# Moving normalisation, last sums and the tanh of a convolution-attention kernel to other engines

## The chip, the cores and the metric

The kernel runs on one core of one Trainium2 chip, all in fp32. The metric is the device time of one execution in microseconds (us), as a median of several runs. The engines are named PE (TensorE), ScalarE (ACT), VectorE (DVE), GpSimd (POOL) and SP (the DMA queue).

## The reference

Eight images of 128 channels by 36 x 36 pixels go through two layers. This is what the changed places compute, cut from the reference:

```python
# layer 0: x = x + conv_attn(groupnorm(x)); only a_x, the first half of the stack, reaches h
x = conv1x1(inp, w_x) + b_x
attn = softmax(einsum('ancq,bncd->anbqd', q, k), axis=-1)      # 1296 queries, 1156 keys
a_x = einsum('bncd,anbqd->anbcq', v, attn)
h = tanh(conv1x1(concat([x, a_x]), w_h) + b_h)
out = conv1x1(h, w_o) + b_o
# layer 1, tokens t = pixels: additive attention
q, k = x @ Wq.T + bq, x @ Wk.T + bk                            # x = layernorm(t)
scores = einsum('bijd,d->bij', tanh(q[:, :, None] + k[:, None]), w) + bw
t = t + softmax(scores) @ x
# then a gated mixture of 64 experts on layernorm(t): per image and expert the top 8 tokens
logits = layernorm(t) @ gate_w.T + gate_b
```

The additive attention is by far the most work: 1296 x 1296 pairs of tokens times 128 channels of tanh, for each image.

## The kernel before, in words

**The main loop.** The kernel turns each tanh of a sum into a quotient: exponentials of sums and differences of channels are made once per token ("features"), matmuls over them give a denominator and a numerator for pairs of tokens, and the sum over channels is a sum of numerator over denominator. An image is cut into 3 query chunks of 432 and 11 key tiles (ten of 128, a remainder of 16). A query chunk with a key tile is a *unit*. A full unit has 12 *slots*, a remainder unit 3; an image has 33 units or 369 slots, the whole kernel 2952. In a slot PE makes two numerators (`n`, in a pool of four PSUM buffers) and, three slots ahead (`LAG`), two denominators (`d`, a pool of two); ScalarE takes the logarithm of the denominators (L815) and, for two slots at a time, the exponential of its negative (L818); VectorE multiplies it with the numerators (L835 to L846); GpSimd adds up two thirds of the products (`accp`, L851 and L853) and VectorE the rest (`accd`).

**Everything else is background.** The other work is written as Python generators that give way after each step. A step is put either at the start of a slot (`step`, `TAKE`: work for VectorE, ScalarE, GpSimd) or behind its matmuls (`matmuls`: work for PE), and says how many slots to rest. Four lanes hold them: the next query features, the attention's end (`attend`) with the last image's gate, the gate of the image before (`gating`), and the background proper, which prepares the next image: `normal`, `conv_keys`, `layer0`, `tokens`, `keys`. `matmul_turn` lets background matmuls in against a budget of `PACE` columns a slot; unused budget is not saved beyond one slot's. The order on each engine is fixed when the program is built, and every engine works its own list in order. The first image's preparation runs before the loop with nothing beside it (`drain`); the experts run after it.

**The places that are touched.**
- `layer0`: for each chunk of 432 queries ten score tiles are exponentiated, five pairs of matmuls give `pa`, summed on VectorE into `ax` (L395, L397). Then `pt` holds the softmax sums, ScalarE makes their reciprocal `ri` by a logarithm and an exponential (L405, L406), and VectorE multiplies and adds `px` into `hpre` (L412, L413). After the third chunk one tanh takes all of `hpre`, which needs another table of functions than the loop's:

```python
            yield step(2)
            nc.scalar.activation(hp, hp, AF.Tanh, bias=hb)
            nc.scalar.preload_act_table_set(LNEXP)
            yield matmuls(2)
```

- `tokens`: transposes bring `r` into token rows (`tpl`), VectorE copies them to `tok`, eleven pairs of statistics follow (L525, L526), GpSimd takes the power -1/2 (L218) and normalises eleven tiles (L538), two per step; then they are transposed back (`tpc`).
- `attend`: each of twelve pieces per image is summed in two halves of PSUM, added in `sums` (L625, L628), and divided and added to the residual by L631, whose inputs `sums` and `t2` lie in SBUF.
- `gate_logits`: twelve tiles are transposed and stored (`tt`), normalised on GpSimd (L681), transposed again and multiplied by the gate. For the last image this is done chunk by chunk.

Of the kernel before, what the change touches and what calls it, by code (L numbers as in the profile page):

```python
# [15 lines left out]
N = H * W  # L16
# [5 lines left out]
T = 108  # L22
# [35 lines left out]
DVE_PAIRS = (2, 5, 8, 11)  # L58
PACE = 370

# [4 lines left out]
def kernel(  # L65
# [55 lines left out]
    with ExitStack() as loop, ExitStack() as score:  # L121
# [83 lines left out]
        hb = const.tile([C, 1], F32, tag="hb", name="hb")  # L205
        nc.vector.tensor_add(hb, ph[:, :1], bh_s)

        LNEXP = "natural_log_exp_and_others"
# [21 lines left out]
        def matmuls(rest=0):  # L230
            return (True, rest)
# [97 lines left out]
        def layer0(b):  # L329
# [16 lines left out]
            for g in range(0, NDT, 4):  # L346
# [14 lines left out]
                yield matmuls()  # L361
            hp = big_tile("hpre")[:, :N]
            for c in range(NCH):
# [12 lines left out]
                for o, n in DTILES:  # L376
# [8 lines left out]
                    yield matmuls()  # L385
                ax = chunk_tile("ax0")
                for j0 in range(0, NDT, 2):
                    pa = aux("pa0")
                    for j in (j0, j0 + 1):
                        n = DTILES[j][1]  # L390
                        bmm(pa[:, :CH], vw[:n, j, :], ex[j][:n], start=(j == j0), stop=(j > j0))
                    yield TAKE
                    if j0 == 0:
                        total(NDT - 1)
                        nc.vector.tensor_scalar(ax, pa[:, :CH], 1.0 / D, None, ALU.mult)  # L395
                    else:
                        nc.vector.scalar_tensor_tensor(  # L397
                            ax, pa[:, :CH], 1.0 / D, ax, ALU.mult, ALU.add
                        )
                    yield matmuls()  # L400
                pt = aux("pt0")
                bmm(pt[:, :CH], ones[:DT], tot[:DT], start=True, stop=True)
                yield TAKE
                ri = chunk_tile("ri0")
                nc.scalar.activation(ri, pt[:, :CH], AF.Ln, scale=1.0 / D)  # L405
                nc.scalar.activation(ri, ri, AF.Exp, scale=-1.0)  # L406
                yield matmuls(1)
                px = aux("px1")
                bmm(px[:, :CH].rearrange("p (a b) -> p a b", b=W), wh_s[:, 0, :],
                   xpad[:, 1 + c * RC : 1 + (c + 1) * RC, 1 : 1 + W], start=True, stop=True)  # L410
                yield TAKE
                nc.vector.tensor_mul(ax, ax, ri)  # L412
                nc.vector.tensor_add(hp[:, cols], px[:, :CH], ax)  # L413
                yield matmuls()
            yield step(2)
            nc.scalar.activation(hp, hp, AF.Tanh, bias=hb)
            nc.scalar.preload_act_table_set(LNEXP)
            yield matmuls(2)
            for c in range(NCH):
                cols = slice(c * CH, (c + 1) * CH)  # L420
                po = aux("po0")
                bmm(po[:, :CH], wo_s, hp[:, cols], start=True, stop=True)
                yield TAKE
                nc.vector.scalar_tensor_tensor(
                    r[:, cols], po[:, :CH], bo_s, r[:, cols], ALU.add, ALU.add
                )
                yield matmuls()
# [63 lines left out]
        def tokens(b):  # L491
# [42 lines left out]
            nc.gpsimd.memset(xh[:, :, C : C + 1], 1.0)  # L534
            yield step()
            for t in range(NKT):
                n = KT[t][1]
                nc.gpsimd.tensor_scalar(  # L538
                    xh[:n, t, :C], tok[:n, t, :], mv[:n, t, 0:1], rs[:n, t : t + 1],
                    ALU.subtract, ALU.mult,  # L540
                )
                if t % 2 == 1:
                    yield step()
            xT = big_tile("xT")[:, :N]
# [56 lines left out]
        def attend(b, c, es):  # L601
# [8 lines left out]
            for i in range(TPC):  # L610
# [3 lines left out]
                for some in (range(6), range(6, NKT)):  # L614
# [9 lines left out]
                    if j < NKT - 1:  # L624
                        nc.vector.tensor_copy(sums, pa)  # L625
                        yield matmuls()
                    else:
                        nc.vector.tensor_add(sums, pa, sums)  # L628
                inv = small.tile([T, 1], F32, tag="inv", name="inv")
                nc.vector.reciprocal(inv, sums[:, C : C + 1])  # L630
                nc.vector.scalar_tensor_tensor(  # L631
                    t2[:T, at, :], sums[:, :C], inv, t2[:T, at, :], ALU.mult, ALU.add
                )
# [15 lines left out]
        def gate_logits(b, chunks):  # L649
# [499 lines left out]
```

## Time and profile before

| What | us |
|---|---|
| median of 3 runs (lowest, highest) | 6428.76 (6428.02, 6435.07) |
| profiled execution, its own time | 6428.41 |
| its span in the trace | 6426.7 |
| before the first slot | 188 |
| an image in the loop, images 0 to 6 | 763 to 768 |
| the last image | 685 |
| after the last slot | 194 |

Starts and lengths of slots are read from the logarithms L815 in the trace. The profile's busy times say how long an engine had something under way; a matmul that waits in the pipe counts as busy, so PE's share is an upper bound. A group's row gives instructions of one line and shape, their number, total and mean, and then the idle time of the engine in front of them with what ended it. The clock is what the throttle granted PE, 1.00 being full speed. Rows "so many us, [idle, who]" of the timeline merge neighbours of one line.

### The profile page before, as it was taken

Reading aid. Unit: us, or ns where it says so; the run is one execution under the profiler, and the core shown is the slowest. Engines: PE = TensorE matmul, PEld = TensorE weight load, DVE = VectorE, ACT = ScalarE, POOL = GpSimd, SP = SyncE. Lnnn points to the kernel's source line nnn. Section 1 sums busy time; section 2 is a strip of 40 time slices with the busy share of each in tenths; the row PEclk is TensorE's granted clock in tenths of the full one; section 3 lists DMA queues with packets and bytes.
Section 4 is the critical chain, followed back from the end, with each engine's and each line's share of the span. In section 5 each row is a group of like instructions: output and inputs, shape, how many; then the busy total and the mean of one; then the engine's idle time right before and its main releaser. Section 6 shows DMA issues by size and latency. Waiting matters only on the chain.

```text
span 6426.7 us, 106771 instructions
## 1 busy us (share of the span) xinstructions
PE 6054.8 (94%) x40448; PEld 2813.9 (44%) x40448; DVE 4900.4 (76%) x9315; ACT 5354.6 (83%) x5426; POOL 4798.1 (75%) x2966
## 2 busy tenths in 40 slices
PE   8999999999999999999999999999999999999986
PEld 4444444444444444444444444444444444544432
DVE  3687778877788777888788887887778877778862
ACT  1788898888888888888888888888888888989970
POOL 3677777787777877777787787778777787888870
PEclk9999999999999999999999999999999999999997
DMA  0200011000110002100111001100011000100017
GB/s 28 66 31 23 22 63 36 30 24 27 56 46 19 24 27 68 33 26 22 44 47 38 22 23 53 43 32 25 20 63 43 23 24 27 61 26 28 24 66 253
DMA packets 155284, 265.78 MB, mean 41 GB/s; under 512 B 53712, under 2 KB 79824, under 8 KB 154768
## 3 DMA queue, kind: packets, MB, share of 16 engines
q1 hardware_dynamic: 154768, 258.95, 12.5%
q8 instruction: 318, 5.21, 0.3%
q14 instruction: 198, 1.62, 0.1%
HBM read 196.81 MB, written 61.83 MB: 40 GB/s over the span
## 4 chain that ended last, share of the span: by engine, by line
PE 67%; DVE 12%; ACT 7%; issue 7%; POOL 6%; DMA 1%; SPq 0%; POOLq 0%; DVEq 0%; ACTq 0%
PE n L793 30%; PE d L793 10%; PE pc L237 7%; PE pa L237 6%; ACT lq L815 5%; DVE n L840 3%; DVE rp L846 3%; PE s L237 3%; PE pk L237 3%; PE pq L237 2%; DVE accd L842 2%; POOL accp L853 2%; DVE t L631 1%; PE n L800 1%; POOL t L681 1%
## 5 line engine op out<-in xcount | busy, mean ns | idle before, releaser
L853 POOL TENSOR_TENSOR accp<-accp,rp 128x864 f32<-128x864 f32 x1464 | 2965.2, 2025 | 1028.0 <-DVE rp L846 975.3
L793 PE MATMUL n<-qf,kf 32*128 32x432 f32 (+1 forms) x11520 | 3239.2, 579 | 93.4 <-DVE rp L846 47.0
L815 ACT ACTIVATE lq<-d 128x864 f32<-128x864 f32 x2952 | 2552.6, 882 | 690.7 <-PE d L793 643.3
L793 PE MATMUL d<-qf,kf 32*128 32x432 f32 (+1 forms) x11520 | 2876.6, 568 | 21.2 <-ACT lq L815 16.4
L846 DVE TENSOR_TENSOR rp<-n,lq 128x432 f32<-128x432 f32 x3984 | 2202.6, 600 | 623.7 <-PE d L793 399.3
L818 ACT ACTIVATE lq<-lq 128x1728 f32<-128x1728 f32 x1488 | 2429.0, 1632 | 47.1
L793 PEld LDWEIGHTS n<-qf,kf 32*128 32x128 f32 (+1 forms) x11520 | 1167.1, 187 | 1703.4 <-DVE rp L846 586.3
L793 PEld LDWEIGHTS d<-qf,kf 32*128 32x128 f32 (+1 forms) x11520 | 1038.8, 188 | 392.2 <-issue 254.1
L840 DVE TENSOR_TENSOR n<-n,lq 128x432 f32<-128x432 f32 x1440 | 811.7, 608 | 280.1 <-PE n L793 239.2
L842 DVE TENSOR_TENSOR accd<-n,accd 128x432 f32<-128x432 f32 x1440 | 867.4, 602 | 24.7
L851 POOL TENSOR_TENSOR accp<-rp 128x864 f32<-128x864 f32 x264 | 533.8, 2022 | 221.1 <-DVE rp L846 217.5
L237 PE MATMUL pa<-xh,e 128*108 128x129 f32 x1920 | 262.6, 284 | 55.6 <-DVE rp L846 34.7
L860 POOL TENSOR_TENSOR accp<-accp 128x432 f32<-128x432 f32 x264 | 290.8, 1101 | 16.2
L237 PEld LDWEIGHTS pa<-xh,e 128*108 128x108 f32 x1920 | 223.3, 175 | 179.1 <-DVE rp L846 107.4
L594 POOL TENSOR_SCALAR qf<-qf,cs_s 128x432 f32<-128x432 f32 x192 | 262.7, 1374 | 42.0 <-ACT qf L593 42.0
L863 POOL TENSOR_TENSOR accd<-accp,accd 128x432 f32<-128x432 f32 x240 | 265.6, 1107 | 28.5 <-DVE accd L842 10.4
L237 PE MATMUL s<-q,k 128*116 128x432 f32 x480 | 229.8, 570 | 3.3 <-DVE q L260 2.1
L237 PEld LDWEIGHTS pk<-xT,a_k 128*128 128x128 f32 x1408 | 172.2, 193 | 109.8 <-DVE accd L842 27.6
L374 POOL TENSOR_TENSOR tot<-tot,e 116x432 f32<-116x432 f32 x192 | 212.0, 1104 | 6.1
L835 DVE TENSOR_TENSOR accd<-n,lq 128x432 f32<-128x432 f32 x240 | 144.9, 604 | 91.6 <-PE n L793 60.5
L381 ACT ACTIVATE e<-s 116x432 f32<-116x432 f32 x240 | 125.0, 521 | 106.6 <-PE s L237 105.5
L237 PE MATMUL pk<-xT,a_k 128*128 128x128 f32 (+1 forms) x1408 | 203.2, 288 | 2.6 <-DVE accd L842 2.3
(175 smaller groups left out, 4144.4 us busy)
## 6 DMA issues: line engine op xcount, KB each, us to landing
kf<-kd SPq DMA_DIRECT2D x240, 512.0 KB
kd<-ks SPq DMA_DIRECT2D x160, 256.0 KB
w<-in_weight_dram SPq DMA_DIRECT2D x32, 1024.0 KB
x<-in_x_dram SPq DMA_DIRECT2D x8, 648.0 KB
t<-tokd SPq DMA_DIRECT2D x96, 54.0 KB
t2d<-t2T SPq DMA_DIRECT2D x24, 216.0 KB
res<-t2d SPq DMA_DIRECT2D x8, 648.0 KB
out_dram<-res SPq DMA_DIRECT2D x8, 648.0 KB
```

What stands on the lines that cost most here:

```text
L237: mm(out, lhsT, rhs, **kw)
L594: nc.gpsimd.tensor_scalar(qf[:, 1, :], qf[:, 0, :], cs_s[:, q : q + 1], None, ALU.mult)
L793: mm(outs[h][:, :CH], kf[rows[h], q, :], qf_of[b, c, q][rows[h], part, :], start=True, stop=True)
L815: nc.scalar.activation(lq[:, o : o + 2, :], d[:, :, :CH], AF.Ln)
L818: nc.scalar.activation(some, some, AF.Exp, scale=-1.0)
L840: mult(ns[h], ns[h], lq[:, o + h, :])
L842: nc.vector.tensor_add(live["d"], ns[h], live["d"])
L846: mult(rp[:, h, :], ns[h], lq[:, o + h, :])
L851: nc.gpsimd.tensor_add(live["p"], live["r"], rp)
L853: nc.gpsimd.tensor_add(live["p"], live["p"], rp)
L860: nc.gpsimd.tensor_add(s[:, 0, :], s[:, 0, :], s[:, 1, :])
L863: nc.gpsimd.tensor_add(d, s[:, 0, :], d)
```

## The change

- *Normalising by VectorE out of PSUM.* In `tokens` and `gate_logits` the normalised tiles are no longer made from SBUF by GpSimd. The tiles are transposed once more by PE into a PSUM buffer (`tpn`, `tp3`), and VectorE subtracts and multiplies from there. The power -1/2 stays with GpSimd.
- *Last sums within PSUM.* The last partial sum of `attend` and of `layer0`'s `pa` is added in place in PSUM, and the next operation reads it there. `pt` and `ri` move ahead of the last pair of `pa`, and the factor 1/D that was cancelled later is dropped.
- *tanh by exponentials and a logarithm.* For each chunk, with y the argument (cut off at 10): exp(2y), then log(1 + that), then exp of its negative give s = 1/(1 + exp(2y)), and tanh y = 1 - 2s. So `w_o` is multiplied by -2 once at the start, and the column sums of `w_o` are added to its bias. There is no full-width `hpre`; each chunk goes on to its output matmul `po` before the next chunk starts.
- `PACE` rises from 370 to 395 columns a slot.

```diff
-PACE = 370
+PACE = 395
...
+        pw = aux("pw")
+        mm(pw[:, :1], wo_s, ones[:, :1], start=True, stop=True)
+        nc.vector.tensor_add(bo_s, pw[:, :1], bo_s)
+        nc.vector.tensor_scalar(wo_s, wo_s, -2.0, None, ALU.mult)
...
-            hp = big_tile("hpre")[:, :N]
...
                 ax = chunk_tile("ax0")
+                ri = chunk_tile("ri0")
                 for j0 in range(0, NDT, 2):
-                    pa = aux("pa0")
+                    if j0 == NDT - 2:
+                        pt = aux("pt0")
+                        bmm(pt[:, :CH], ones[:DT], tot[:DT], start=True, stop=True)
+                        yield TAKE
+                        nc.scalar.activation(ri, pt[:, :CH], AF.Ln)
+                        nc.scalar.activation(ri, ri, AF.Exp, scale=-1.0)
+                        yield matmuls()
+                    pa = aux("pa0")[:, :CH]
...
-                        nc.vector.tensor_scalar(ax, pa[:, :CH], 1.0 / D, None, ALU.mult)
+                        nc.vector.tensor_copy(ax, pa)
+                    elif j0 < NDT - 2:
+                        nc.vector.tensor_add(ax, pa, ax)
                     else:
-                        nc.vector.scalar_tensor_tensor(
-                            ax, pa[:, :CH], 1.0 / D, ax, ALU.mult, ALU.add
-                        )
+                        nc.vector.tensor_add(pa, pa, ax)
+                        nc.vector.tensor_mul(ax, pa, ri)
                     yield matmuls()
...
-                nc.vector.tensor_mul(ax, ax, ri)
-                nc.vector.tensor_add(hp[:, cols], px[:, :CH], ax)
-                yield matmuls()
-            yield step(2)
-            nc.scalar.activation(hp, hp, AF.Tanh, bias=hb)
-            nc.scalar.preload_act_table_set(LNEXP)
-            yield matmuls(2)
-            for c in range(NCH):
-                cols = slice(c * CH, (c + 1) * CH)
+                nc.vector.tensor_add(px[:, :CH], px[:, :CH], ax)
+                nc.vector.tensor_scalar(ax, px[:, :CH], hb, 10.0, ALU.add, ALU.min)
+                yield step(2)
+                nc.scalar.activation(ax, ax, AF.Exp, scale=2.0)
+                nc.scalar.activation(ax, ax, AF.Ln, bias=1.0)
+                yield step()
+                nc.scalar.activation(ax, ax, AF.Exp, scale=-1.0)
+                yield matmuls(1)
                 po = aux("po0")
-                bmm(po[:, :CH], wo_s, hp[:, cols], start=True, stop=True)
+                bmm(po[:, :CH], wo_s, ax, start=True, stop=True)
...
-            yield step()
-            for t in range(NKT):
-                n = KT[t][1]
-                nc.gpsimd.tensor_scalar(
-                    xh[:n, t, :C], tok[:n, t, :], mv[:n, t, 0:1], rs[:n, t : t + 1],
-                    ALU.subtract, ALU.mult,
-                )
-                if t % 2 == 1:
-                    yield step()
+            yield matmuls()
+            for g in range(0, NKT, 4):
+                tp = aux("tpn")
+                some = list(range(g, min(g + 4, NKT)))
+                for t in some:
+                    o, n = KT[t]
+                    turned_to(tp[:n, (t - g) * C : (t - g + 1) * C], r[:, o : o + n], ident)
+                yield TAKE
+                for t in some:
+                    n = KT[t][1]
+                    nc.vector.tensor_scalar(
+                        xh[:n, t, :C], tp[:n, (t - g) * C : (t - g + 1) * C],
+                        mv[:n, t, 0:1], rs[:n, t : t + 1], ALU.subtract, ALU.mult,
+                    )
+                yield matmuls()
...
-                    else:
-                        nc.vector.tensor_add(sums, pa, sums)
+                nc.vector.tensor_add(pa, pa, sums)
                 inv = small.tile([T, 1], F32, tag="inv", name="inv")
-                nc.vector.reciprocal(inv, sums[:, C : C + 1])
+                nc.vector.reciprocal(inv, pa[:, C : C + 1])
                 nc.vector.scalar_tensor_tensor(
-                    t2[:T, at, :], sums[:, :C], inv, t2[:T, at, :], ALU.mult, ALU.add
+                    t2[:T, at, :], pa[:, :C], inv, t2[:T, at, :], ALU.mult, ALU.add
                 )
...
-                yield matmuls()
-            yield step()
-            for j, t in enumerate(tiles):
-                nc.gpsimd.tensor_scalar(
-                    t2[:T, t, :], t2[:T, t, :], mv[:, t, 0:1], rs[:, j : j + 1],
-                    ALU.subtract, ALU.mult,
-                )
-                if t % 2 == 1:
-                    yield step()
-            yield matmuls(2)
+                yield matmuls(1)
+                tp = aux("tp3")
+                for j in range(TPC):
+                    turned_to(tp[:T, j * C : (j + 1) * C], tt[:, j * T : (j + 1) * T], ident)
+                yield TAKE
+                for j in range(TPC):
+                    t = c * TPC + j
+                    nc.vector.tensor_scalar(
+                        t2[:T, t, :], tp[:T, j * C : (j + 1) * C],
+                        mv[:, t, 0:1], rs[:, t - tiles[0] : t - tiles[0] + 1],
+                        ALU.subtract, ALU.mult,
+                    )
+                yield matmuls(1)
```

More of the change, by code (lines that the diff above doesn't have):

```diff
@@ L386, in layer0 @@
                 ax = chunk_tile("ax0")
+                ri = chunk_tile("ri0")
                 for j0 in range(0, NDT, 2):
-                    pa = aux("pa0")
+                    if j0 == NDT - 2:
[6 more added lines that the diff above has]
+                    pa = aux("pa0")[:, :CH]
                     for j in (j0, j0 + 1):
                         n = DTILES[j][1]
-                        bmm(pa[:, :CH], vw[:n, j, :], ex[j][:n], start=(j == j0), stop=(j > j0))
+                        bmm(pa, vw[:n, j, :], ex[j][:n], start=(j == j0), stop=(j > j0))
                     yield TAKE
@@ L394, in layer0 @@
                         total(NDT - 1)
-                        nc.vector.tensor_scalar(ax, pa[:, :CH], 1.0 / D, None, ALU.mult)
-                    else:
-                        nc.vector.scalar_tensor_tensor(
-                            ax, pa[:, :CH], 1.0 / D, ax, ALU.mult, ALU.add
-                        )
+                        nc.vector.tensor_copy(ax, pa)
+                    elif j0 < NDT - 2:
+                        nc.vector.tensor_add(ax, pa, ax)
+                    else:
+                        nc.vector.tensor_add(pa, pa, ax)
+                        nc.vector.tensor_mul(ax, pa, ri)
                     yield matmuls()
[L401 to L407, printed above, removed]
                 px = aux("px1")
```

## The prediction

> **What bounds the kernel now.** I read the page first, then the stretches between marks, then the waits and the timeline of the stretches that stand out. The page's engine row and clock row:
>
> ```profile
> PE 6054.8 (94%) x40448; PEld 2813.9 (44%) x40448; DVE 4900.4 (76%) x9315; ACT 5354.6 (83%) x5426; POOL 4798.1 (75%) x2966
> PEclk9999999999999999999999999999999999999997
> ```
>
> A TensorE that is 94% busy looks like the bound, but busy time includes waits inside a pipelined matmul, and four engines are above 75%. So I cut the loop. Each of the 2952 slots has one `lq<-d` logarithm on ScalarE (L815); its starts mark slots, twelve slots are one key tile (a "unit"; a remainder tile has three), and 33 units are one image. Images take 763 to 768 us, the last, with nothing to prepare for a next one, 685; 188 us lie before the first slot and 194 after the last. Here are seven stretches from the table of busy time by stretch (columns: stretch, length, busy PE, PEld, DVE, ACT, POOL, granted clock, DMA):
>
> ```profile
> 4854.00:4881.60 27.60, 23.95 (x116) 10.10 (x114) 23.08 (x42) 20.26 (x21) 26.07 (x23) 0.88 0.03 6
> 5381.30:5408.80 27.50, 25.00 (x241) 11.00 (x240) 23.28 (x43) 25.07 (x25) 20.62 (x11) 1.00 0.10 29
> 5408.80:5416.00 7.20, 6.24 (x135) 3.24 (x135) 1.93 (x4) 5.02 (x6) 2.21 (x3) 0.63 0.11 43
> 5416.00:5444.00 28.00, 25.85 (x231) 12.67 (x231) 20.69 (x52) 20.60 (x20) 16.23 (x11) 0.85 0.16 44
> 5444.00:5473.30 29.30, 24.18 (x112) 11.17 (x115) 21.35 (x40) 20.29 (x20) 25.68 (x23) 0.77 0.06 20
> 5498.00:5522.50 24.50, 24.47 (x166) 14.30 (x160) 17.19 (x32) 23.43 (x26) 16.38 (x9) 1.00 0.30 108
> 5722.70:5742.64 19.94, 19.23 (x98) 7.68 (x96) 16.72 (x31) 19.75 (x21) 16.34 (x10) 1.00 0.09 27
> ```
>
> The last row is a unit without other work: 19.94 us, of which ScalarE is busy 19.75. **The bare loop is bound by ScalarE.** The row above is a unit with a full share of key features: PE 24.47 of 24.50. Rows 1 and 5 are stretches in which GpSimd is busy 26 of 28 or 29 us and the clock falls: gate normalisation (L681) and token normalisation (L538). Rows 2 to 4 hold the long tanh. So the loop is balanced, and a few stretches per image stand far above it. The tanh, on ScalarE's timeline, and what it does to PE:
>
> ```profile
> 5404.83 1.28 ACT L416 ACT_TABLE_LOAD   x1
> 5406.13 1.38 ACT L416 ACTIVATE hpre<-hpre,hb 128x1296 f32<-128x1296 f32 x1
> 5407.52 1.28 ACT L417 ACT_TABLE_LOAD   x1
> 5409.76 1.11 PE L800 MATMUL d<-qf,kf 64*32 64x108 f32 x64 [3.12 <-ACT lq L815]
> ```
>
> ScalarE is away for 3.97 us, PE idles 3.12, and the next 7.2 us row runs at a clock of 0.63. The token normalisation, on GpSimd's timeline:
>
> ```profile
> 5449.46 2.14 POOL L218 TENSOR_TENSOR ln_rs<-ve,neg_half 128x11 f32<-128x11 f32 x1
> 5451.61 2.02 POOL L853 TENSOR_TENSOR accp<-accp,rp 128x864 f32<-128x864 f32 x1
> 5453.62 1.57 POOL L538 TENSOR_SCALAR xh<-tok,ln_mv,ln_rs 128x128 f32<-128x128 f32 x2
> 5468.36 8.35 POOL L853 TENSOR_TENSOR accp<-accp,rp 128x864 f32<-128x864 f32 x4
> ```
>
> The small operations stand between the accumulations; the last row is a backlog of four accumulations run without a gap, while VectorE waited 4.6 us for an `rp` buffer.
>
> **What the Trainium skill says.** "TensorE: Matmul & The Clock Gate", Part 1: an idle window of about 3.4 us halves the PE clock. The trace agrees in kind: after the 3.12 us of idleness it shows half clock for 13.65 us. "ScalarE: Activation LUTs", What ACT_TABLE_LOAD costs: about 1283 ns each; measured 1.28. "SBUF — State Buffer", Who interferes with whom: a VectorE instruction with two SBUF inputs contends with a GpSimd instruction that reads SBUF, and the later one blocks. The trace shows it for the division by the softmax sum, whose three forms differ only by where GpSimd stands:
>
> ```profile
> L631 DVE SCALAR_TENSOR_TENSOR t<-sums,inv,t 108x128 f32<-108x128 f32 x96 | 87.9, 915 | 29.0 <-DMA t<-tokd 25.7
> L631 DVE SCALAR_TENSOR_TENSOR t<-sums,inv,t x96: 350/674/1841, 456.6 to 6274.5; 108x128 f32<-108x128 f32 x96
> ```
>
> 350 ns is the minimum, seen at the end where GpSimd rests; 1841 is about one accumulation more.
>
> **A rule for an undisturbed unit.** From 119 undisturbed units of this trace I fitted: unit = 20.0 + 0.36 x background PE + 0.40 x extra ScalarE + 0.35 x extra VectorE + 0.09 x extra GpSimd (us; 1.67 ns per fp32 column, half for a transpose; rms 0.8). It gives 736 us for an image that takes 765. The excess is named: 7.3 in the token unit (29.3 for 22.0), 10.9 in the three tanh rows (62.7 for 51.8), 4.9 in the gate unit (27.6 for 22.7), and some 6 in the top-8 unit and the remainder tiles, which the change leaves alone.
>
> **The change part by part, per image, images 0 to 6.**
> - *Normalising.* 23 GpSimd operations of 0.79 us (18.2 us) go. 23 transposes come, at 0.17 to 0.18 us (the tp and tpl groups, 32.1/192 and 14.4/80): 4.0 us of PE. 23 VectorE operations out of PSUM come, at 0.29 (the 108x129 copy L625, 288 ns): 6.7 us. By the rule: 4.0 x 0.36 + 6.7 x 0.35 - 18.2 x 0.09 = +2.1.
> - *Tanh.* 3.97 us of ScalarE go. Nine activations of 0.52 to 0.56 come, 0.09 less each where they overlap a neighbour: 4.1. Nothing by the rule. VectorE gets one operation more per chunk, 3 x 0.61 x 0.35 = +0.6. In place of one block of 4 us there are three of 1.1 and three of 0.5, each behind two slots of rest.
> - *Excess.* 7.3 + 10.9 + 4.9 = 23.1 loses its cause. What is late next is VectorE, which keeps eleven pairs of statistics (0.27 + 0.18) beside the new work; I let 3 of it stay: -20.
> - *Sums in PSUM.* Twelve L631 fall from 0.915 to about 0.35, since one input is PSUM: 6.8 us of VectorE, -2.4. They hold a score buffer longer by about 0.5 us; I take nothing, since PE's wait there is 0.3 us a time. The in-PSUM adds elsewhere replace operations of equal size (608 ns).
> - *A wait added.* The first `xh` operation on VectorE now waits for `ln_rs` from GpSimd, asked for one slot earlier. GpSimd owes 2.02 + 2.14 + 0.12 us there, a slot is 2: +2.5, with two multiplications, and so PE's next numerators, queued behind. Bounds 0 and 6 (a clock dip in its wake). In the gate, three slots lie between: nothing.
> - *Pace 395.* In the built program's order a whole image's background ends earlier, but the new rests put a remainder tile (unit 16) without any background. In the last image, each of three such tiles is followed by a dip, and the units behind the two plain ones take 22.15 and 24.09 for 19.94: +3. The fuller units, and emptier last two, are in the rule: applied to the changed order it gives 739 for 736, against +2.7 from the items above. Bounds of this item: 0 and 8.
> - DMAs: none is added; the queue's `xr` copy waits for `xh`, which comes earlier.
>
> Sum per image: 2.7 - 20 - 2.4 + 2.5 + 3 = -14.2, seven times -99. *Last image:* its three gate stretches take 29.3, 28.7 and 28.6 where the rule gives 22; the chain transpose, normalise, transpose, gate matmul stays, so I take -5 each: -15. *Before the loop* nothing hides: per chunk PE now waits through four VectorE operations (2.6) and three activations (1.9), less the 0.7 of px: 3.9 x 3 = 11.7, for 3.25 before; and the eleven L538 (8.7) become 2.8 on VectorE, about 5.5 sooner: +3. *The tail:* 3.1 us of L681 against four transposes and four VectorE operations, -1. Together -112. The profiled execution took 6428.41 us (span 6426.70), the median 6428.76, so both sums agree: **6316 us**.
>
> **Rivals.**
> 1. *All excess goes, no new wait* (0.16): -17.3 -2.4 = about -20 an image, -140, last image -20: **6270**. For: GpSimd is visibly the longest in rows 1 and 5. Against: VectorE is at 23 of 27.6 there already.
> 2. *The stall changes hands* (0.14): half of the 20 stays, since VectorE becomes the late one and the clock still drops; -4 an image, -28, and -8 in the last image: **6393**. For: row 1's VectorE plus 3 us more.
> 3. *The chunk ends become three small tanhs* (0.06). Each has some five slots with no background in which PE waits for a chain over VectorE, ScalarE and PE. If every one costs the 10.9 of the tanh rows, 33 come where 10.9 left: -14 + 33 - 3 = +16 an image, -15 for the last: **6525**. It decides against the change from about 6 us per chunk end. Against: no block over 1.1 us, and PE idled 3.12 before the clock fell.
> That the division or the scaling does not do what it says is excluded by the code: every changed operation stands in the built order.
>
> **How the numbers follow.** The likeliest case (0.64) gives 6316, its own range 6280 to 6365. Range 6265 to 6394: it takes in rivals 1 and 2, the bounds of the two added waits (7 x 3.5 and 7 x 5 us) and leaves out rival 3 and the far edges. A measurement of this kernel tells 0.2% (13 us) from no change. Faster 0.91, within it 0.04, slower 0.05.
>
> **What would show it.** Right: POOL near 4650 us; no table load in the loop; L631's successor near 350 ns throughout; the 13.65 us half clock per image gone; token and gate units at 23 to 25. Wrong: half clock at each chunk end; a wait of VectorE on `ln_rs` over 5 us; units of the new chunk ends above 27.

## The result, and the profile after

| | before | after |
|---|---|---|
| median, us | 6428.39 | 6345.7 (6345.15 to 6352.28) |
| ratio to before, 95% interval | 1 | 0.9873 (0.9856 to 0.989) |
| span of the profiled execution, us | 6426.7 | 6343.6 |
| its mean granted clock | 0.966 | 0.973 |

The change saves 83 us. The forecast was 112 us less, 6316, so the direction and the range were right and the middle was 29 us too low. Cut by the same slot marks as before (each unit starts at its first `lq` logarithm, now L829), the 83 us fall as follows. Units are counted 0 to 32 in an image; 5, 16 and 27 are the remainder tiles. Here the last image is taken to the end of its last slot, some 1.6 us later than in the table of the kernel before.

| Stretch | before | after | change | forecast |
|---|---|---|---|---|
| before the first slot | 188.2 | 197.9 | +9.7 | +3 |
| an image, mean of images 0 to 6 | 765.7 | 755.8 | -9.9 (7 x: -69) | -14.2 (7 x: -99) |
| ... its gate units 2 to 5 | 81.8 | 81.9 | +0.1 | |
| ... its end of layer 0 and tokens, units 25 to 29 | 115.0 | 109.7 | -5.3 | |
| ... its other units | 568.9 | 564.1 | -4.8 | |
| the last image | 686.5 | 665.2 | -21.3 | -15 |
| after the last slot | 192.3 | 190.1 | -2.2 | -1 |

The engine row and the clock row of the page of the kernel after:

```profile
PE 6093.4 (96%) x40634; PEld 2834.7 (45%) x40634; DVE 4918.1 (78%) x9525; ACT 5365.8 (85%) x5474; POOL 4657.2 (73%) x2782
PEclk9999999999999999999999999999999999999997
```

GpSimd fell by 141 us to 4657, as forecast near 4650, and VectorE rose by 18 only, because the cheaper division pays for most of its new work. The time does not follow either sum. Here are the stretches of image 6 that answer to those shown of before, in the table of busy time by stretch (columns: stretch, length, then busy PE, PEld, DVE, ACT, POOL, granted clock, DMA share, GB/s). They are units 2 and 3 (gate), units 26, 27 and 28 (end of layer 0; statistics; normalisation and the `tpc` transposes), unit 29 (keys), and the gate stretch of the last image's first chunk (its unit 13):

```profile
4779.60:4807.00 27.40, 26.18 (x122) 12.30 (x120) 26.03 (x55) 20.42 (x20) 18.57 (x10) 0.88 0.11 36
4807.00:4829.20 22.20, 22.00 (x121) 10.08 (x120) 21.35 (x46) 20.27 (x20) 17.43 (x11) 1.00 0.07 17
5331.00:5353.20 22.20, 19.81 (x168) 9.30 (x163) 20.30 (x47) 21.36 (x24) 16.45 (x10) 1.00 0.19 55
5353.20:5363.10 9.90, 9.90 (x205) 5.38 (x205) 8.84 (x22) 5.18 (x7) 5.83 (x4) 0.56 0.17 55
5363.10:5390.10 27.00, 27.00 (x255) 15.28 (x255) 20.99 (x43) 20.94 (x21) 19.25 (x14) 0.85 0.08 22
5390.10:5415.80 25.70, 25.45 (x169) 14.99 (x168) 17.27 (x31) 24.17 (x29) 16.01 (x9) 1.00 0.32 113
5761.60:5784.50 22.90, 21.62 (x118) 9.27 (x116) 22.34 (x45) 20.27 (x20) 17.36 (x10) 1.00 0.09 33
```

The tanh unit (third row) came down from 27.5 to 22.2 us, and unit 29, which held the token normalisation before, from 29.3 to 25.7; the normalisation now lies in unit 28, which takes 27.0. The gate gained next to nothing. Before, its normalising filled unit 3 (27.6 us, GpSimd busy 26.1), and unit 2 ahead of it took 22.5. Now most of it stands in unit 2: unit 3 fell to 22.2 and unit 2 rose to 27.4, in which GpSimd is busy 18.6 and **VectorE 26.0**. The remainder tile (fourth row) runs at a clock of 0.56 and takes 9.9 us for 7.2. The gate stretch of the last image's first chunk, where less else runs, fell from 28.7 to 22.9.

The groups of VectorE that the change made or touched (columns: line, engine, operation, output and inputs, shape, count; busy us, mean ns of one; idle time ahead of them and what ended it):

```profile
L642 DVE SCALAR_TENSOR_TENSOR t<-pa,inv,t 108x128 f32<-108x128 f32 x96 | 33.7, 351 | 27.2 <-DMA t<-tokd 23.7 <-DVE inv L641 0.3
L696 DVE TENSOR_SCALAR t<-tp,t_mv,t_rs 108x128 f32<-108x128 f32 x96 | 32.6, 401 | 1.3 <-PE tp L245 1.3
L551 DVE TENSOR_SCALAR xh<-tpn,ln_mv,ln_rs 128x128 f32<-128x128 f32 (+1 forms) x88 | 29.9, 404 | 33.5 <-POOL ln_rs L222 24.1 <-PE tpn L245 9.3
L295 DVE SCALAR_TENSOR_TENSOR dev<-dev,gn_mv 128x1 f32<-128x1 f32 x8 | 11.8, 1470 | 0.3
L217 DVE TENSOR_SCALAR ve<-t_mv 108x12 f32<-108x12 f32 (+1 forms) x10 | 11.4, 1144 | 0.0
L217 DVE TENSOR_SCALAR ve<-ln_mv 128x11 f32<-128x11 f32 x8 | 9.7, 1216 | 0.3
```

The division is at 351 ns in the mean, for 915. The new normalising operations take 400 ns each, and 340 when four follow each other (1.37 us for four on the timeline), where 288 had been assumed. And three lines that the change does not touch stand out by their mean: adding an epsilon to 11 or 12 numbers per partition takes 1.1 to 1.2 us, a square of one number 1.5.

VectorE's timeline in the token stretch (start, length, operation, count, [idle before it, who ended it]) shows the wait that the forecast had added, and one of those small operations:

```profile
5356.59 1.36 DVE L217 TENSOR_SCALAR ve<-ln_mv 128x11 f32<-128x11 f32 x1
...
5365.63 1.37 DVE L551 TENSOR_SCALAR xh<-tpn,ln_mv,ln_rs 128x128 f32<-128x128 f32 x4 [3.07 <-POOL ln_rs L222]
```

And GpSimd's in the same place:

```profile
5355.91 2.01 POOL L867 TENSOR_TENSOR accp<-accp,rp 128x864 f32<-128x864 f32 x1 [3.69 <-DVE rp L860]
...
5362.40 1.09 POOL L877 TENSOR_TENSOR accd<-accp,accd 128x432 f32<-128x432 f32 x1
5363.46 2.14 POOL L222 TENSOR_TENSOR ln_rs<-ve,neg_half 128x11 f32<-128x11 f32 x1
```

`ve` starts at 5356.59 under an accumulation that ends at 5357.92, and is done at 5357.95. `ln_rs` is asked for early but stands behind three more additions in GpSimd's list (the one shown at 5362.40 is the last of them), ends at 5365.60, and VectorE's `xh` starts there, 3.07 us late.

### The profile page after: what moved, and what is told of

Its sections match the earlier page's. It is cut to its first block, busy times and chain, and to the rows that moved or that the text cites. A ratio compares the mean times of both kernels' runs of the same rounds, so it can differ in the third digit from the quotient of the medians.

```text
span 6343.6 us, 107262 instructions
## 1 busy us (share of the span) xinstructions
PE 6093.4 (96%) x40634; PEld 2834.7 (45%) x40634; DVE 4918.1 (78%) x9525; ACT 5365.8 (85%) x5474; POOL 4657.2 (73%) x2782
## 4 chain that ended last, share of the span: by engine, by line
PE 70%; DVE 11%; ACT 8%; issue 7%; POOL 2%; SPq 1%; DMA 1%; DVEq 0%; ACTq 0%; POOLq 0%
PE n L807 31%; PE d L807 10%; PE pc L241 8%; PE pa L241 7%; ACT lq L829 6%; DVE n L854 4%; PE s L241 3%; DVE rp L860 3%; PE pk L241 2%; PE pq L241 2%; DVE accd L856 2%; PE n L814 1%; PE d L814 1%; POOL accp L867 1%; PE px L241 1%
## 5 line engine op out<-in xcount | busy, mean ns | idle before, releaser
L807 PE MATMUL n<-qf,kf 32*128 32x432 f32 (+1 forms) x11520 | 3233.4, 575 | 51.6 <-DVE accd L856 25.1
L829 ACT ACTIVATE lq<-d 128x864 f32<-128x864 f32 x2952 | 2566.1, 882 | 592.1 <-PE d L807 517.0
L807 PE MATMUL d<-qf,kf 32*128 32x432 f32 (+1 forms) x11520 | 2846.0, 562 | 24.8 <-ACT lq L829 19.7
L807 PEld LDWEIGHTS d<-qf,kf 32*128 32x128 f32 (+1 forms) x11520 | 1016.5, 186 | 412.9 <-issue 229.8
L241 PE MATMUL pa<-e,vw 116*128 116x432 f32 x480 | 203.1, 549 | 1.6 <-DVE accd L856 0.2
```

The costliest lines, as they stand in the source:

```text
L241: mm(out, lhsT, rhs, **kw)
L807: mm(outs[h][:, :CH], kf[rows[h], q, :], qf_of[b, c, q][rows[h], part, :], start=True, stop=True)
L829: nc.scalar.activation(lq[:, o : o + 2, :], d[:, :, :CH], AF.Ln)
```

## The experiments

All ratios are against the kernel before, measured beside it on the same chip; they have an uncertainty of 0.1 to 0.2%, so a difference of less than 10 to 15 us between two versions is not clear. A single profiled execution can lie up to 12 us from its median (that of `sums_only` lies 11.5 above), so sums over stretches are read as such.

### The parts one at a time

*`pace_only`: the kernel before with*

```diff
-PACE = 370
+PACE = 395
```

> The kernel before with PACE 395 alone. Theory (the budget only moves background earlier): fuller slots cost what the emptier ones at the end of an image give back, or a little less, 0 to +12 us against before (6428), +5 taken. Rival A (the higher budget itself is a gain, because steps that wait in their lanes get through sooner): -15 us or more. Rival B (fuller slots stall VectorE and ScalarE): over +20 us.

Measured: 6431.25 us, ratio 1.0002 (0.9993 to 1.0011). The pace alone moves nothing.

*`norm_only`: the pace and both normalisations, tokens' and gate's, as in the diff of the change; the sums and the tanh as before.*

```diff
-                nc.gpsimd.tensor_scalar(xh[:n, t, :C], tok[:n, t, :], ...)
+                    turned_to(tp[:n, ...], r[:, o : o + n], ident)
+                    nc.vector.tensor_scalar(xh[:n, t, :C], tp[:n, ...], ...)
```

> The kernel before with the two normalisations moved to PE and VectorE, and PACE 395; tanh and sums as before. Theory (GpSimd's backlog was the stall in the token and gate units): about -55 us against before: some -7 an image, -12 in the last image, -6 before the loop, +5 for the pace. The unit of the token normalisation falls from 29.3 us to 25 or less. Rival (VectorE takes over the stall, with its wait on ln_rs and the added operations): -15 us or less of a gain, most of it in the last image and before the loop.

Measured: 6424.29 us, 0.9991 (0.9982 to 0.9999). Of the part that was to carry most, 4 us came, for 55 expected; it is the rival's case. Images 0 to 6 last 768.6 us in the mean, `pace_only`'s 767.0; only the last image (666.1 for 674.6) and the time before the loop (183.9 for 188.4) gained. The stretches of image 6 of `pace_only`, units 2, 26 and 28, by busy time:

```profile
4837.36:4861.73 24.37, 20.24 (x116) 9.37 (x112) 24.09 (x48) 20.41 (x21) 21.91 (x15) 1.00 0.14 49
5400.10:5425.64 25.54, 24.02 (x166) 11.07 (x159) 23.48 (x58) 20.32 (x21) 19.30 (x13) 0.80 0.16 47
5431.38:5462.36 30.98, 29.25 (x267) 15.40 (x263) 17.87 (x33) 22.68 (x25) 24.33 (x19) 0.83 0.12 44
```

and the same units of `norm_only`:

```profile
4842.21:4869.62 27.41, 25.60 (x125) 12.37 (x120) 26.34 (x55) 20.54 (x20) 18.57 (x10) 0.88 0.10 36
5406.18:5436.51 30.33, 25.95 (x174) 12.34 (x169) 25.65 (x69) 20.65 (x21) 18.73 (x12) 0.83 0.14 40
5442.48:5469.10 26.62, 26.04 (x279) 14.94 (x279) 17.48 (x32) 23.41 (x26) 16.64 (x11) 1.00 0.21 72
```

The unit with the old normalisation did fall, 30.98 to 26.62, and its clock is whole again. The unit in front of it, where the statistics, the wait for `ln_rs` and the new `xh` now stand together, rose from 25.54 to 30.33, VectorE from 23.5 to 25.7 of it. The gate units did the same: unit 2 rose by 3.0, unit 3 fell by 4.2. **The stall changed hands**: it is the mechanism of the second rival, and for these two parts nothing of the gain was left, where the forecast had let 3 of 20 us stay.

*`tanh_only`: the pace and all edits in `layer0` (tanh, `pt` and `ri` earlier, its last sum in PSUM); normalising and `attend` as before.*

```diff
-            nc.scalar.activation(hp, hp, AF.Tanh, bias=hb)
-            nc.scalar.preload_act_table_set(LNEXP)
+                nc.scalar.activation(ax, ax, AF.Exp, scale=2.0)
+                nc.scalar.activation(ax, ax, AF.Ln, bias=1.0)
+                yield step()
+                nc.scalar.activation(ax, ax, AF.Exp, scale=-1.0)
```

> The kernel before with the tanh made of exponentials and a logarithm, chunk by chunk (with the moved pt and ri and the last pa sum in PSUM), and PACE 395. Theory: -15 us against before: about -4 an image, +10 before the loop, +5 for the pace; no half clock of 13.65 us at the end of layer0. Rival (the three chunk ends cost as much as the one tanh did): +10 to +20 us, all of it before the loop and from the pace.

Measured: 6396.15 us, 0.9944 (0.9925 to 0.9962), -32 us for -15 expected. In the loop an image gains 7.2 us on `pace_only` (759.8 for 767.0), 5.1 of it in units 25 to 29. Before the loop it loses 14.9 (203.3 for 188.4). PE's timeline there shows the loss, in the kernel after:

```profile
106.08 1.81 PE L241 MATMUL po<-ax,w_o 128*128 128x432 f32 x2 [3.96 <-ACT ax L425]
107.68 8.57 PE L241 MATMUL pc<-xpad,wq_t 128*128 128x432 f32 x18
```

and of the kernel before, the same convolution, which followed without a wait:

```profile
102.39 6.69 PE L237 MATMUL pc<-xpad,wq_t 128*128 128x432 f32 x18
```

The wait of 3.96 us is what the forecast had worked out (3.9). The convolution behind it takes 8.57 us for 6.69, since the clock stands at 0.50 from 104.6 to 111.4; the same dip, 6.8 us long, starts at 135.4 and 166.1, behind the other two chunk ends. So each of three chunk ends costs the wait and a clock dip: 5.0 us a chunk instead of the 2.8 forecast (11.7 less 3.25, by three).

*`sums_only`: the kernel before with `attend`'s last sum in PSUM, `PACE` at 370.*

```diff
-                        nc.vector.tensor_add(sums, pa, sums)
+                nc.vector.tensor_add(pa, pa, sums)
...
-                    t2[:T, at, :], sums[:, :C], inv, t2[:T, at, :], ALU.mult, ALU.add
+                    t2[:T, at, :], pa[:, :C], inv, t2[:T, at, :], ALU.mult, ALU.add
```

> The kernel before (PACE 370) with the last sums of the attention left in PSUM. Theory (the division by the softmax sum had two SBUF inputs and waited for GpSimd; it falls from a mean of 915 ns to 350): 12 x 0.565 us of VectorE an image, of which a third counts: about -19 us. Rival (VectorE has slack there, or the longer hold of the PSUM buffer eats it): 0 +- 6 us with the 350 ns seen all the same.

Measured: 6378.68 us, 0.9923 (0.9907 to 0.9939): -50 us, the largest part of all, for -19 expected. Its division takes 351 ns too; the size was right and the exchange rate wrong. An attention unit (unit 12 of image 4) in the busy times of the kernel before:

```profile
3522.50:3548.10 25.60, 22.82 (x158) 13.01 (x157) 24.35 (x49) 20.34 (x21) 16.34 (x9) 1.00 0.09 25
```

and in those of `sums_only`:

```profile
3502.30:3524.50 22.20, 21.95 (x157) 12.90 (x157) 20.14 (x49) 20.24 (x20) 16.39 (x9) 1.00 0.09 29
```

VectorE was busy 24.35 of 25.60 us, the most of the five engines in this unit. The groups of the division in the two stretches, of the kernel before:

```profile
L631 DVE SCALAR_TENSOR_TENSOR t<-sums,inv,t 108x128 f32<-108x128 f32 x3 | 5.0, 1664 | 0.1
```

and of `sums_only`:

```profile
L630 DVE SCALAR_TENSOR_TENSOR t<-pa,inv,t 108x128 f32<-108x128 f32 x3 | 1.1, 351 | 0.1
```

The three divisions that stand here took 1.66 us each, not the mean 0.915. They gave VectorE 3.9 us and the unit 3.4. Over an image, twelve divisions by 0.565 us are 6.8 us, and the units outside gate and layer-0 end lost 5.8 (568.9 to 563.1), where a third was expected. Unit 12 is not alone in this. Without it, the units of images 0 to 6 that hold divisions gave VectorE 3.9 us an image and became 4.0 shorter, though VectorE was busy only 70 to 92% of them. So a full VectorE is not needed for a saving to count nearly whole.

That the division waited for GpSimd can be read from the kernel before: of its 96 divisions 56 take over 0.4 us, and each of these starts under a GpSimd operation and ends 0.15 us after it.

Normalising, tanh and sums alone give -4, -32 and -50, together -86 us (the pace is in two of them and worth nothing by itself), near the whole's -83. The sum is no proof that the parts don't meet: the tokens' normalising is worth more in company, as `after_old_tok` shows.

### Taking parts of the kernel after away or moving them

*`after_late_xh`: two slots of rest ahead of the `tpn` transposes in `tokens`.*

```diff
             nc.gpsimd.memset(xh[:, :, C : C + 1], 1.0)
-            yield matmuls()
+            yield matmuls(2)
```

> The changed kernel with one edit: two slots of rest between the power of -1/2 on GpSimd and the token transposes, so that VectorE does not stand at its first normalisation until ln_rs is there (3.07 us in the trace of the changed kernel). Theory (VectorE is the late engine in the token stretch and its wait counts whole): the wait falls under 0.5 us and the kernel takes some 2 us less an image, about 6332 us (the changed kernel: 6346). Rival (the two slots of rest, which no background matmul fills, cost as much as the wait): 6346 +- 6.

Measured: 6330.71 us, 0.985 (0.9835 to 0.9865), 15 less than the kernel after. That is at the edge of what the two intervals tell apart; `best_a` below adds the same edit to `after_eps_pool` and takes 21 us less than it. From the list of waits (engine, line, waited for: us in total, times, longest) of the kernel after:

```profile
DVE xh L551 <- POOL ln_rs L222: 24.1, 8, 3.5
```

and of this kernel:

```profile
DVE xh L551 <- POOL ln_rs L222: 2.3, 1, 2.3
```

The wait was 3.0 us in the mean, 2.5 forecast; 21.8 us of it went, some 15 of which show in the time. So most of VectorE's stop there was on the path.

*`after_eps_pool`: the epsilon of the token and gate statistics, and the square of `dev`, on GpSimd; `dev` reads the mean out of PSUM.*

```diff
-            nc.vector.tensor_scalar(ve, var, eps, None, ALU.add)
+            eng = nc.vector if shape[1] == 1 else nc.gpsimd
+            eng.tensor_scalar(ve, var, eps, None, ALU.add)
...
-            nc.vector.tensor_sub(dev, mv[:, 0:1], gm)
-            nc.vector.scalar_tensor_tensor(dev, dev, dev, mv[:, 1:2], ALU.mult, ALU.add)
+            nc.vector.tensor_sub(dev, mv[:, 0:1], pm[:, :1])
+            nc.gpsimd.tensor_mul(dev, dev, dev)
+            nc.gpsimd.tensor_add(dev, dev, mv[:, 1:2])
```

> The changed kernel with the small VectorE operations that work from SBUF to SBUF in the normalisations moved to GpSimd: the two additions of epsilon (ve, 1.25 and 1.36 us each in the loop against 0.17 with GpSimd at rest) and the second half of the group norm's dev (1.47 us on average, 0.22 at the least). Theory (they stand blocked behind GpSimd's accumulations, in stretches where VectorE has no gap, so their 3.5 us an image count whole): about 20 to 25 us less than the changed kernel, near 6324. Rival (only a third counts, as in the recorded rule): -8, near 6338; or GpSimd is the late one with its new operations: 6346 or more.

Measured: 6312.64 us, 0.982 (0.9803 to 0.9836), 33 less than the kernel after, for 20 to 25 expected. The groups on GpSimd that took most of the work over:

```profile
L218 POOL TENSOR_SCALAR ve<-ln_mv 128x11 f32<-128x11 f32 x8 | 2.1, 268 | 16.6 <-DVE ln_mv L534 16.6
L218 POOL TENSOR_SCALAR ve<-t_mv 108x12 f32<-108x12 f32 x7 | 1.8, 259 | 0.0
L296 POOL TENSOR_TENSOR dev<-dev 128x1 f32<-128x1 f32 x8 | 1.6, 196 | 16.7 <-DVE dev L295 16.7
```

About 33 us of VectorE (11.8 + 11.4 + 9.7, the groups above) became some 8 of GpSimd, so this saving too counted whole and not by a third. The gate units fell from 81.9 to 78.6 an image. With the timeline above (`ve` ends with the accumulation under it), this agrees with "SBUF — State Buffer", Who interferes with whom, in the Trainium skill: of a VectorE and a GpSimd instruction that both need the port pair they share, the first to issue holds it for its whole length and the other blocks; it counts a `tensor_scalar` from SBUF to SBUF, as `ve` is, among those that can need it.

*`after_gate_last`: the old GpSimd normalisation in the gates of images 0 to 6; the last image's stays in PSUM.*

```diff
+                if b < NB - 1:
+                    yield matmuls()
+                    continue
...
+            if b < NB - 1:
+                yield step()
+                for j, t in enumerate(tiles):
+                    nc.gpsimd.tensor_scalar(t2[:T, t, :], t2[:T, t, :], ...)
```

> The changed kernel with the gate's normalisation given back to GpSimd in images 0 to 6; the last image keeps PE and VectorE. Theory (in images 0 to 6 VectorE is full in that stretch, units 2 and 3 together take 49.6 us after and 50.1 before, so the move gains nothing there): 6346 +- 10. Rival (the recorded excess of 4.9 us in the gate unit was a gain of the move): +30, near 6376.

Measured: 6352.7 us, 0.9877 (0.9858 to 0.9896), not told apart from the kernel after. Where the next image is prepared beside it, it does not matter which engine normalises the gate's tokens (images 0 to 6 take 755.7 us each for 755.8). Its one trace has the last image at 680.0 for 665.2. The gate of an image runs in the slots of the next, so the old normalisation of image 6 stands there: units 2 to 6 of the last image take 113.1 us for 98.0, as much as the whole difference. With nothing to prepare beside it the move to VectorE does gain, by this one trace; the median is only 7 us above.

*`after_old_tok`: the block in `tokens` as before, everything else changed.*

```diff
-                    nc.vector.tensor_scalar(xh[:n, t, :C], tp[:n, ...], ...)
+                nc.gpsimd.tensor_scalar(xh[:n, t, :C], tok[:n, t, :], ...)
```

> The changed kernel with the token normalisation given back to GpSimd (two tiles a step, from SBUF). Theory (with VectorE the late engine, the move is worth its 5 us before the loop and about nothing an image): 6351, between 6340 and 6362. Rival (the recorded excess of 7.3 us in the token unit was GpSimd's backlog, and comes back): +45, near 6395.

Measured: 6372.43 us, 0.9921 (0.99 to 0.9941), 27 more than the kernel after, between the two expectations (6351 and 6395). 5.7 of it lie before the loop and 18 in images 0 to 6 (2.6 each). So the tokens' normalisation does pay once the long tanh is gone from in front of it.

### Adding up

*`locks_only`: the kernel before with the edits of `sums_only` and `after_eps_pool`.*

> The kernel before (PACE 370, normalising on GpSimd, one tanh) with two edits: the last sums of the attention in PSUM, and the additions of epsilon and the second half of dev on GpSimd. No VectorE operation of these then has all its inputs in SBUF. Theory (what the change really took away is VectorE standing behind GpSimd's reads): the sums alone gave -50, epsilon and dev gave some -33 in the changed kernel; here some -70, near 6360, close to the whole change. Rival (epsilon and dev paid only because VectorE had been given the normalising): -50, near 6378.

Measured: 6384.2 us, 0.9931 (0.9915 to 0.9948), no better than the sums alone. The expected 70 did not come. Moving `ve` and `dev` is worth 33 us in the kernel after and nothing in the kernel before. The rival is right. A reason would be that GpSimd is busy 26 of 28 us in the gate and token units there, so that a longer list on GpSimd is paid; that is argued, and the units don't show it: units 2 to 5 take 82.7 us an image in `locks_only` as in `sums_only`, units 25 to 29 take 113.1 for 114.6.

*`best_a`: the kernel after with the edits of `after_late_xh` and `after_eps_pool`. `best_b`: `best_a`, and the token statistics two pairs a slot, not three:*

```diff
-                if t % 3 == 2:
+                if t % 2 == 1:
```

> The changed kernel with both edits that gained alone: epsilon and dev on GpSimd, and two slots of rest ahead of the token transposes. Theory (they act in different stretches and add up: -33 and -15): 6298, between 6290 and 6310. Rival (both only decide whether the clock falls in the token stretch): 6313, no more than the better one.

> As the one with both edits, and the token statistics spread over more slots: two pairs a slot in place of three. Theory (the burst of statistics on VectorE, up to 2.4 us, starves PE until its clock falls in the remainder unit; shorter bursts avoid some of it): 3 us less an image than without, near 6280. Rival (the burst only moves; PE has no background there either way): as without, 6298 +- 6.

Measured: `best_a` 6291.48 us, 0.9786 (0.9771 to 0.9801): 15 and 33 add up, with -54 against the kernel after. `best_b` 6279.85 us, **0.9763 (0.9749 to 0.9778)**, the fastest of all. Its busy times in image 6, units 2, 27, 28 and 29:

```profile
4716.96:4740.06 23.10, 22.76 (x117) 10.01 (x116) 22.81 (x53) 20.36 (x20) 19.09 (x13) 1.00 0.13 42
...
5286.89:5292.76 5.87, 5.63 (x210) 3.21 (x208) 5.66 (x19) 5.01 (x6) 4.14 (x3) 1.00 0.28 92
5292.76:5318.10 25.34, 23.33 (x238) 11.66 (x231) 21.34 (x46) 20.71 (x22) 20.81 (x15) 0.93 0.08 23
5318.10:5343.40 25.30, 25.16 (x162) 13.94 (x161) 18.67 (x35) 23.65 (x27) 16.80 (x10) 1.00 0.24 84
```

The gate unit is 23.1 for 27.4, the remainder tile 5.87 at full clock for 9.9 at 0.56. The spread statistics are what mends the remainder tile: over images 0 to 6 it takes 9.1 us in the kernel after, 8.3 in `best_a` and 6.3 in `best_b`, with a dip in seven, six and one of the seven images. Units 2 to 5 take 77.9 an image and units 25 to 29 take 103.3, against 81.9 and 109.7 in the kernel after: here is most of the excess that the forecast had counted as gone.

*`best_c`: `best_b`, with the three activations and the output matmul of chunk c put into the convolution of chunk c + 1.*

```diff
+                for i, says in enumerate(conv_turns(wq_t, (c * RC, RC), 0, 0, W, q)):
+                    yield says
+                    if c > 0 and i == 3:
+                        nc.scalar.activation(ax, ax, AF.Exp, scale=2.0)
+                        nc.scalar.activation(ax, ax, AF.Ln, bias=1.0)
+                    elif c > 0 and i == 5:
+                        nc.scalar.activation(ax, ax, AF.Exp, scale=-1.0)
+                if c > 0:
+                    yield from output(c - 1, ax)
```

> As the one with both edits and the spread statistics, and for two of the three chunks the activations of the tanh and the output matmul are put among the next chunk's convolution of queries instead of ahead of it. Theory (before the loop PE no longer stands for the chain of two chunks, 3.9 us each; in the loop some five slots a chunk get background): -8 before the loop, -2 an image, about -20 against the one without. Rival (the rests of a chunk end cost nothing in the loop): -8.

Measured: 6309.16 us, 0.9813 (0.9798 to 0.9827), 29 slower than `best_b`. Before the loop it does more than expected, 184.1 us for 199.9 (-8 expected): the half clock behind both chunk ends goes with the wait. This is PE's timeline there, no wait and a convolution of 6.69 us:

```profile
102.52 0.89 PE L242 MATMUL px<-xpad,w_h 128*128 128x432 f32 x2
103.25 6.69 PE L242 MATMUL pc<-xpad,wq_t 128*128 128x432 f32 x18
```

But an image lasts 752.3 for 745.1, and 6.2 of these 7.2 us lie in units 25 to 29. With the rests gone, the background ends earlier and unevenly: in image 6 two of its units, 25 and 31, get 131 and 5 background columns a slot (transposes counted half) where `best_b` has 288 and 224, and the difference goes to others. That the uneven spread is the cause is argued, not shown: `PACE` was not set anew for this version.

## Why the prediction was right or wrong

- **Direction and range: right, the total partly by luck.** The removed work stood in the stretches that were too long, and no rival on the slower side came whole. But two large errors cancel. The sums gave 50 us where 17 were forecast, and the excess fell short. With the sums at their 17, the kernel would stand near 6379 (an estimate: the measured 6346 and the 33 us more of `sums_only`), nearer to the second rival's 6393 than to 6316.
- **Sums in PSUM, -2.4 us an image: the term mis-sized most, on the good side.** The 6.8 us saved on VectorE were put through the rule's mean coefficient, 0.35. They counted nearly whole: 3.4 of 3.9 in unit 12, and 50 us in the median (38 in the one trace, which lies above its median). Why a blocked operation costs more than the rule has for VectorE's work is open. A full VectorE is not it alone, as the other units show; that one long stop holds up PE's buffers is a rival that no run tested.
- **Excess, -20 us an image: the step that failed, for the normalising.** "Loses its cause" took GpSimd's 26 of 28 us for the only cause, though the first rival's "against" and the second rival both named VectorE. Of the 7.3 and 4.9 us of the token and gate units nothing came when normalising moved alone (`norm_only` 768.6 an image, `pace_only` 767.0). In the whole, the gate gave nothing (units 2 to 5 +0.1; `after_gate_last` the same time an image) and the tokens 2.6 (`after_old_tok`). The tanh rows' 10.9 gave 7.2 (`tanh_only`). `norm_only` shows how: the cleared unit gains 4.4 us, the one ahead of it loses 4.8.
- **What stood in its place.** The operations took 0.34 to 0.40 us, not 0.29; and `ve` and `dev`, which the forecast did not list, cost 1.1 to 1.5 us each where VectorE had become the late engine. Moving them gave 33 us, while in the kernel before it gave none. Together with VectorE's 26.0 of 27.4 us in unit 2 this says that VectorE took the place of GpSimd as the late engine.
- **The half clock of 13.65 us at the end of layer 0: gone, as said, but another came.** In image 6 the clock is at half for 17 us from 5354.3, over the remainder tile (0.56 in the fourth row) and into unit 28, in the wake of statistics that run six pairs together on VectorE; PE is busy 1.84 us of the 2.90 ahead of it, and its longest idle stretch there is 1.06 us. "TensorE: Matmul & The Clock Gate", Part 1, in the Trainium skill says that the gate follows how busy PE has lately been, and this agrees; the idle window of about 3.4 us that the prediction takes from it does not, since PE was never idle that long here. `best_b`, with two pairs a slot, has no half clock in its remainder tile in six of seven images. Over an image, the time at half clock fell from 38 us to 26, and to 11 in `best_b`.
- **The wait on `ln_rs`, +2.5 us an image: right.** 3.0 on VectorE; taken away, it gave 15 us of 6346, 2.1 an image.
- **Remainder tile without background, +3 us: not seen as described.** Pace alone gave +1.3 an image and -11.9 in the last image, in the sum nothing. In image 6 of the kernel after unit 16 keeps one background matmul, and over images 0 to 6 it and the unit behind it run at 1.00 and 0.99 of the clock. The empty tile is unit 27, with a single transpose. Emptiness alone is not enough for a dip there: in `pace_only` it has none at all in images 1 to 6, and full clock.
- **Before the loop, +3 us, measured +9.7.** The normalisation's part was right (-4.5 for -5.5), and the wait at each chunk end too (3.96 for 3.9). What lacked was the clock dip behind the wait: the tanh costs 14.9 for 8.5. A half clock at each chunk end was among the prediction's signs of being wrong; here, before the loop, it came.
- **Last image and tail: near, but not for the reason given,** -21.3 for -15 and -2.2 for -1. The gate stretches there (units 3, 13 and 24) are at 22.4 to 22.9 us, the 22 of the rule, so the whole excess went and not 5 of 7. But of the 21.3 the pace alone gives 11.9 in its one trace (`pace_only`: 27.6, 25.1 and 25.1 us in these units), which was not forecast, and normalising 8.5 more (`norm_only`: 22.0, 22.6 and 22.6).
- **The first rival** (all excess gone, 6270) is what `best_b` comes near to in time, at 6280, but that kernel has three more edits to VectorE's work and is no support for the rival. The third rival did not come in the loop: image 6's unit 26 with the last chunk's end takes 22.2 us, and the units of the three chunk ends (17, 20 and 26) keep 0.96 to 0.99 of the clock over images 0 to 6.
- **Signs.** GpSimd near 4650 us, no table load in the loop and 350 ns for the division came as forecast. Gate and token units at 23 to 25 us did not: units 2 and 28 take 27.4 and 27.5 in the mean of images 0 to 6.

Open is why moving the tokens' normalisation pays 27 us beside the other parts and almost nothing alone. The traces show that without the new tanh its statistics and `xh` fall into the unit behind the long tanh; an experiment that only moves them apart was not made.

## What to carry to other kernels

Before pricing saved or added work, read which engine is full in the very unit where it stands: a microsecond of VectorE spent blocked behind GpSimd counted nearly whole here, where a third had been fitted for its work in undisturbed units. Moving work from the late engine to the one that is next late moves the stall; look then for what else on the new engine can go, here operations on a dozen numbers that cost over a microsecond each. Where PE has nothing beside it, price a wait together with the half clock that follows it. And check which term of a forecast earned a good total: here a saving three times its size hid a gain that did not come.

## What was not expected of the hardware

- Adding one number to 128 x 11 values takes VectorE 1.36 us under a GpSimd accumulation of 2.01 us and 0.17 us with GpSimd idle (in `norm_only`, image 6); GpSimd does it in 0.27.
- The same division takes 0.35 us in all 96 cases when its first input lies in PSUM, and 0.35 to 1.84 when it lies in SBUF. All 56 slow ones end 0.15 us after the GpSimd operation under which they began.
- The clock fell to half after 2.9 us in which PE was still busy for 1.84: complete idleness was not needed.
- Half clock comes in steps: in every trace each stretch of it, but for the one at the trace's end, lasts a whole multiple of 3.41 us, in the kernel after's image 6 for example 17.1 (5 steps) and before its loop three times 6.8 (2 steps).
